# A state-space mixer on one core: where the second gate product, the step sizes' product and ScalarE's exponentials stand in the order

## The chip, the cores and the metric

The kernel runs on one core of one Trainium2 chip. A core has five engines with queues of their own: TensorE (PE in the profile; its weight loads are PEld), VectorE (DVE), ScalarE (ACT), GpSimd (POOL) and SyncE (SP, which issues the DMAs here). The metric is the device time of one launch in microseconds (us). Products are written to PSUM, from where DVE or ACT copy them out.

## The reference

One layer of attention over 32x32 tokens, a layer of two state-space mixers (forward and backward), and a spectral convolution. The change lies in the mixers, each of which computes this, for 8 sequences of 1024 tokens:

```python
def _mamba3(x, in_proj, conv_w, conv_b, A_log, dt_bias, D, norm_w, out_proj):
    zxbcdt = x @ in_proj
    z, xbc, dt = jnp.split(zxbcdt, [D_INNER, D_INNER + CONV_DIM], axis=-1)
    xp = jnp.pad(xbc, ((0, 0), (K - 1, 0), (0, 0)))
    conv = sum((xp[:, i:i + l, :] * conv_w[:, i] for i in range(K))) + conv_b
    xbc = jax.nn.silu(conv)
    xh, Bm, Cm = jnp.split(xbc, [D_INNER, D_INNER + D_STATE], axis=-1)
    dt = jax.nn.softplus(dt + dt_bias)
    A = -jnp.exp(A_log)
    y = _ssd(xh, dt, A, Bm, Cm) + xh * D[None, None, :, None]
    yg = y.reshape(b, l, D_INNER) * jax.nn.silu(z)
    yn = yg * jax.lax.rsqrt(jnp.mean(yg * yg, -1, keepdims=True) + EPS) * norm_w
    return yn @ out_proj
```

`_ssd` works in chunks of 64 tokens: decays are exponentials of differences of running sums of dt*A, each chunk's state is B times the decayed x, the states are passed on from chunk to chunk, and y is a sum of the product within the chunk and that with the state before it.

## The kernel before

All is in float32. The mixer stage is a loop over 16 units: sequence b = 0 to 7, and in each direction d = 0 (forward, the even units) and d = 1 (backward, the odd ones). The order of the instructions on every engine is the order in which the program writes them (`manual_schedule` with all engines in order), so an instruction that waits holds all behind it on its engine. One pass of the loop handles three units at once: it ends the one before (`last`), does the core of the present one (`u`), and prepares the next (`following`).

The steps of a pass, by the names that the profile shows, in the order before the change:

- `take_decays(following)`: the exponentials of the next unit's running sums (tiles cums, rest, dec, L817 to L823), and five DMAs on SP that spread them (lm and ec from cd). `between(u, Exp)`: the exponentials of lm (L857), 128x2048 in two halves.
- `turn_x(u)`: x is transposed on PE (sx, L954), and DVE multiplies it by the step sizes (xdt). `turn_b(u)`: B is transposed and multiplied with C on PE (sb, L971), and ACT copies both out (bg, L979).
- In an even unit with a sequence b+1 still to come (`fresh`), `turn_tokens` transposes its normalized tokens (px) and ACT copies them (bxt, L475).
- `project_x`/`copy_x` for the next unit, two halves: products pp on PE (L870), copies xp on ACT (L890). `gate(last)`: y times the gates on DVE, squares on ACT (L1092).
- `decayed_x(u)`, `weigh_decays(u)` on DVE (xdd, lm). `end(last)` on PE: the out-projection spo (L1099), the square sums misc (L1111) and their turn (L1125); from these rms_v on DVE, rms on POOL (L1129), and `scale_rows` on ACT (L1137), eight instructions that read spo.
- `steps(fresh)`: the step sizes, a generator that the loop advances: product pd on PE (L493), softplus in pieces on DVE and ACT (sp_v, sp_e, sp_u, sp_l), then dt and da.
- `project_z`/`activate_z`, two halves: products pz, gates zs on ACT with Silu (L916). `chunk_states` (pst, L1001), `pass_states` on DVE (state, L1018) with four DMAs (moved).
- `convolve` (three taps on DVE for each half, L903), `from_row` (lm on POOL, L848), `activate_x` (Silu on ACT, L908), `between(following, Relu)` (L857), `project_bc` (pb, L925) and `activate_bc` (bt and ct, L941). `outputs(u, 0)` and `outputs(u, 1)`: y, in two halves (sy, L1066), with the decays `add_decays` (pdec) of the unit after next between them in even units.
- In odd units the tokens of sequence b+2 are normalized (`normalize`, `normalized`: b_shift on DVE, ln_x on ACT, L460).

PSUM is handed out in two pools of two halves each[...]: `ps_w` for sx, sb, px, pp, pd, pz, pb and pdec, `ps_s` for spo, misc, pst and sy. A new tile takes a half only when the last reader of the tile before in it is done:

```python
        ps_w = s.enter_context(tc.tile_pool(name="b_ps_w", bufs=2, space=PSUM))
        ps_s = s.enter_context(tc.tile_pool(name="b_ps_s", bufs=2, space=PSUM))
```

[...]a load (ACT_TABLE_LOAD) stands where the function changes between Silu, Exp and Ln.

Of the kernel before, what the change touches and what calls it, by code (L numbers as in the profile page):

```python
# [45 lines left out]
def fast_kernel(ctx: ExitStack, tc: tile.TileContext, a: dict, out: bass.AP, bad: bass.AP):  # L46
# [431 lines left out]
    def steps(b, seq, pd):  # L478

        xt = seq["xt"]

        def small(tag):
            return tokens.tile([P, NT, n2], F32, tag=tag, name=f"{tag}{b}")

        def wide(t):
            return t.rearrange("p d h -> p (d h)").unsqueeze(1).to_broadcast([P, NT, n2])

        pd = pd[:, : NT * n2].rearrange("p (j h) -> p j h", j=NT)
        for j in range(NT):
            nc.tensor.matmul(  # L493
                pd[:, j, :],
                lhsT=xt[:, pad + j * P : pad + (j + 1) * P],
                rhs=wdt.rearrange("p d h -> p (d h)"),
                start=True,
                stop=True,
            )
        v = small("sp_v")  # L500
        nc.vector.tensor_tensor(v, pd, wide(dtb), ALU.add)
        e = small("sp_e")
        nc.vector.tensor_scalar(e, v, -1.0, None, ALU.mult)
        nc.vector.tensor_tensor(e, e, v, ALU.min)
        nc.scalar.activation(e, e, AF.Exp)
        yield
        u = small("sp_u")
        nc.vector.tensor_scalar(u, e, 1.0, None, ALU.add)  # L508
        lg = small("sp_l")
        nc.scalar.activation(lg, u, AF.Ln)  # L510
        yield
        nc.vector.scalar_tensor_tensor(u, u, -1.0, e, ALU.add, ALU.subtract)
        nc.vector.tensor_tensor(lg, lg, u, ALU.subtract)
        dt = small("dt")
        nc.vector.scalar_tensor_tensor(dt, v, 0.0, lg, ALU.max, ALU.add)
        da = tokens.tile([P, 2, NH, NT], F32, tag="da", name=f"da{b}")
        nc.vector.tensor_tensor(
            da.rearrange("p d h j -> p j d h"),
            dt.rearrange("p j (d h) -> p j d h", d=2),
            nega.unsqueeze(1).to_broadcast([P, NT, 2, NH]),  # L520
            ALU.mult,
        )
        seq["dt"], seq["da"] = dt, da
# [4 lines left out]
    with ExitStack() as s:  # L528
# [182 lines left out]
        for n in range(len(units) + 2):  # L711
# [28 lines left out]
            elif n in (103, 119):  # L740
                norming = normalized(n // 112, bridge, *norm)
                next(norming)
            elif n in (105, 122):
                next(norming, None)
            elif n == 113:
                turn_tokens(0, seqs[0], ps_t.tile([P, T], F32, tag="t", name="px0"))
            elif n == 117:
                sizes = steps(0, seqs[0], ps_t.tile([P, T], F32, tag="t", name="pd0"))
                next(sizes)
            elif n in (121, 123):  # L750
                next(sizes, None)
        assert not [*mixing, *making, *going, *coming]
# [9 lines left out]
    with ExitStack() as s:  # L762
# [431 lines left out]
        for at, u in enumerate(units):  # L1194
# [4 lines left out]
            early_decays = after_it and u.d == 1  # L1199
            if following and u.d == 1:  # L1200
                turn_decays(following)
            if at == 0:
                between(u, AF.Relu, 1.0)
            if following:
                take_decays(following)
            between(u, AF.Exp, -1.0)
            turn_x(u)
            weigh_start(u, u.convolved)
            if last:
# [1 line left out]
            turn_b(u)  # L1211
            if fresh:
                turn_tokens(fresh, seqs[fresh], wide_psum(ps_w, f"px{fresh}"))
            if following:
                project_x(following, 0)
                copy_x(following, 0)
# [3 lines left out]
            if following:  # L1220
                project_x(following, 1)
                copy_x(following, 1)
            if early_decays:
                add_decays(after_it)
            decayed_x(u)
            weigh_decays(u, 0)
            if last:
                end(last)
            if early_decays:
                turn_decays(after_it)  # L1230
            if following:
# [4 lines left out]
            norm = None  # L1236
            if u.d == 1 and b < B:
                norm = normalize(bridge, b, later=True)
            going = iter(())
            if fresh:  # L1240
                going = steps(fresh, seqs[fresh], wide_psum(ps_w, f"pd{fresh}"))
                next(going)
            weigh_decays(u, 1)
            if following:
                convolve(following, 0, range(pad - 1))
            next(going, None)
            for n in range(2):
                project_z(u, n)
                activate_z(u, n)
            if following:  # L1250
                first_tap(following, 1)
            if norm:
# [6 lines left out]
            chunk_states(u)  # L1259
            pass_states(u)  # L1260
            next(going, None)
            norming = normalized(b, bridge, *norm) if norm else iter(())
            next(norming, None)
            if stored:
                reload(stored)
            stored = None
            if following:
                convolve(following, 0, range(pad - 1, pad))
                activate_x(following, 0)
                between(following, AF.Relu, 1.0)  # L1270
                project_bc(following)
                activate_bc(following)
                convolve(following, 1)
            outputs(u, 0)
            if after_it and not early_decays:
                add_decays(after_it)
            if following:
                activate_x(following, 1)
            next(norming, None)
            outputs(u, 1)  # L1280
            if last:
                add_rows(last)
# [1076 lines left out]
```

## Time and profile before

| | us |
|---|---|
| median of 3 runs | 1477.29 |
| lowest, highest run | 1474.59, 1480.68 |
| the profiled execution | 1471.66 |
| its span, first to last instruction | 1469.9 |
| PE busy in it | 1340.2 (91%) |
| DVE busy | 1095.4 (75%) |
| ACT busy | 912.9 (62%) |
| POOL busy | 505.9 (34%) |

The mixer's first unit begins with its turned x (sx) at 474.3 us of the span, the last one's at about 1009. The mean granted clock of PE over the span is 0.978 of full speed. Busy times of PE overlap within the engine and are no measure of its distance from its peak; what its queue waits for is told by the list of waits, where each line has the waiting engine, tile and line, what it waited for, the sum, the number of waits and the longest. In lines in order of time the first two numbers are start and duration in us, the arrow points from what is read to what is written, and the brackets give the idle time before and what ended it. "issue" is a wait for which the profile shows no cause.

### The profile page before, as it was taken

To read this page: it belongs to the slowest core of one execution; us is meant where nothing else is said; L and a number is where in the kernel's file an instruction comes from. 1 tells how busy PE (TensorE), PEld (TensorE's weight loads), DVE (VectorE), ACT (ScalarE), POOL (GpSimd) and SP (SyncE) were. 2 spreads that over 40 slices of the span, in tenths; PEclk is the share of its full clock that TensorE was granted. 3 is DMA by queue.
4 is the path that set the end of the run, shared out by engine and by line. 5 is a ranking of instruction groups with operands and counts; after the bars stand their busy time and mean duration, and the time that the engine had idled before them with its cause. 6 is when DMAs were issued, how large, how long until landed. Compare 5 with 4: busy or idle time off the path is not lost. (4 is left out here: it accounts for less than half of the span.)

```text
span 1469.9 us, 45286 instructions
## 1 busy us (share of the span) xinstructions
PE 1340.2 (91%) x19782; PEld 841.3 (57%) x19782; DVE 1095.4 (75%) x2138; ACT 912.9 (62%) x1421; POOL 505.9 (34%) x510
## 2 busy tenths in 40 slices
PE   5999999999998889998989899998599899999977
PEld 2323333333333556665656566655489899999963
DVE  6788888788767687878787877787555577777755
ACT  3766666766765777777777777666355455555520
POOL 3336966866201332323232323233186211111100
PEclk9999999999999999999999999999799999999989
DMA  7101111110002334444444444341258422322258
GB/s 182 35 1 30 44 36 37 51 50 9 8 1 58 74 73 98 92 91 96 90 95 90 92 91 97 88 90 29 69 191 218 128 76 68 91 71 76 68 144 322
DMA packets 139382, 123.09 MB, mean 84 GB/s; under 512 B 44808, under 2 KB 118152, under 8 KB 135080
## 3 DMA queue, kind: packets, MB, share of 16 engines
q1 hardware_dynamic: 137064, 115.93, 30.8%
q10 hardware_dynamic: 2112, 4.19, 0.7%
q8 instruction: 157, 2.57, 0.7%
q14 instruction: 49, 0.40, 0.1%
HBM read 78.15 MB, written 34.08 MB: 76 GB/s over the span
## 5 line engine op out<-in xcount | busy, mean ns | idle before, releaser
L633 ACT ACTIVATE pr<-pt 128x1024 f32<-128x1024 f32 x256 | 247.9, 1021 | 114.3 <-PE pt L628 112.7
L658 DVE TENSOR_TENSOR two<-pr,pr 128x1024 f32<-128x1024 f32 x128 | 162.8, 1312 | 20.7 <-ACT pr L633 19.8
L1433 ACT COPY gs<-pg 128x512 f32<-128x512 f32 x256 | 132.5, 602 | 63.4 <-PE pg L1420 47.5
L1431 DVE COPY gs<-pg 128x512 f32<-128x512 f32 x256 | 158.8, 684 | 14.1 <-PE pg L1420 8.9
L628 PE MATMUL pt<-q,k 32*128 32x512 f32 x1024 | 159.3, 653 | 7.0 <-ACT pr L633 4.7
L1420 PE MATMUL pg<-taps,mst 32*128 32x128 f32 x4096 | 145.2, 280 | 4.4 <-ACT gs L1433 3.5
L1420 PEld LDWEIGHTS pg<-taps,mst 32*128 32x128 f32 x4096 | 133.3, 188 | 16.4 <-issue 11.4
L649 PE MATMUL po<-pr,v 128*32 128x512 f32 x1024 | 139.3, 602 | 0.0
L925 PE MATMUL pb<-bxt,wbc 128*128 128x512 f32 x256 | 115.6, 604 | 14.7 <-ACT zs L916 14.7
L1454 PE MATMUL py<-gs,u 128*32 128x128 f32 (+1 forms) x4096 | 127.8, 277 | 0.2 <-DVE gs L1431 0.2
L861 POOL TENSOR_TENSOR ec<-ec,ct 128x2048 f32<-128x2048 f32 x16 | 72.6, 4536 | 153.1 <-ACT ct L941 141.0
L903 DVE SCALAR_TENSOR_TENSOR xs<-xp,cw,xs 128x1024 f32<-128x1024 f32 x96 | 121.8, 1282 | 4.6 <-issue 1.7
L1454 PEld LDWEIGHTS py<-gs,u 128*32 128x32 f32 (+1 forms) x4096 | 112.0, 140 | 7.5 <-DVE gs L1431 0.4
L1443 POOL TENSOR_SCALAR u<-u 128x512 f32<-128x512 f32 x16 | 24.0, 1497 | 227.2 <-DMA u<-ud 120.1
L628 PEld LDWEIGHTS pt<-q,k 32*128 32x128 f32 x1024 | 47.6, 186 | 85.5 <-issue 32.3
L1129 POOL TENSOR_TENSOR rms<-rms_v,mhalf 128x8 f32<-128x8 f32 x16 | 27.9, 1742 | 187.5 <-DVE rms_v L1127 187.5
L925 PEld LDWEIGHTS pb<-bxt,wbc 128*128 128x128 f32 x256 | 47.7, 191 | 73.1 <-issue 59.1
L1018 DVE SCALAR_TENSOR_TENSOR state<-state,dec,pst 128x64 f32<-128x64 f32 x448 | 87.3, 275 | 1.1
L848 POOL TENSOR_TENSOR lm<-cs,lm 128x2048 f32<-128x2048 f32 x16 | 57.9, 3621 | 60.6 <-DVE sp_u L508 30.8
L649 PEld LDWEIGHTS po<-pr,v 128*32 128x32 f32 x1024 | 27.7, 109 | 88.2 <-issue 84.1
L1099 PE MATMUL spo<-wo,y 128*128 128x128 f32 x512 | 71.0, 288 | 7.9 <-DVE y L1091 7.8
L957 DVE TENSOR_TENSOR xdt<-sx,dt 128x1024 f32<-128x1024 f32 x32 | 37.9, 1220 | 52.9 <-PE sx L954 52.9
(278 smaller groups left out, 2797.9 us busy)
## 6 DMA issues: line engine op xcount, KB each, us to landing
lm<-cd SPq DMA_DIRECT2D x32, 512.0 KB
ec<-cd SPq DMA_DIRECT2D x32, 512.0 KB
ud<-sp SPq DMA_DIRECT2D x8, 1024.0 KB
u<-ud SPq DMA_DIRECT2D x32, 256.0 KB
yd<-sums SPq DMA_DIRECT2D x32, 256.0 KB
moved<-state SPq DMA_DIRECT2D x48, 128.0 KB
yt<-yd SPq DMA_DIRECT2D x6, 1024.0 KB
X<-in_x SPq DMA_DIRECT2D x8, 512.0 KB
```

What stands on the lines that cost most here:

```text
L628: nc.tensor.matmul(pt[:, i, :], lhsT=k[rows, j * P : (j + 1) * P], rhs=q[rows, cols], start=True, stop=True)
L633: nc.scalar.activation(pr[:, 2 * g : 2 * g + 2, :].rearrange("p i t -> p (i t)"), pt.rearrange("p i t -> p (i t)"), AF.Exp, scale=SCALE,)
L649: nc.tensor.matmul(po[rows, :], lhsT=vs[b][:, j, rows], rhs=pr[:, h, :], start=(j == 0), stop=(j == NT - 1))
L658: nc.vector.tensor_tensor(two, sums["pr"][:, 2 * g : 2 * g + 2, :], pr[:, 2 * g : 2 * g + 2, :], ALU.add)
L861: t = nc.gpsimd.tensor_tensor(u.ec, u.ec, u.ct.unsqueeze(1).to_broadcast([P, NH, NT, L]), ALU.mult)
L903: u.convolved = nc.vector.scalar_tensor_tensor(acc, xp[:, at : at + T], cw[u.d][:, n, i : i + 1], acc, ALU.mult, ALU.add)
L925: nc.tensor.matmul(u.pb[:, i * 512 : (i + 1) * 512], lhsT=wbc[u.d][:, k, :], rhs=xt[:, at : at + 512], start=(k == 0), stop=(k == KC - 1),)
L1018: nc.vector.scalar_tensor_tensor(u.state[:, k, h, :], u.state[:, k - 1, h, :], u.dec[:, c, h, j : j + 1], u.pst[c][:, j, h, :], ALU.mult, ...
L1420: nc.tensor.matmul(pts[g][:, e, :], lhsT=mst[rows, n * 4 + e, :], rhs=taps[rows, cols].rearrange("p f q m i -> p (f q m i)"), start=True, ...
L1431: nc.vector.tensor_copy(to, frm)
L1433: nc.scalar.copy(to, frm)
L1454: nc.tensor.matmul(py[t * 32 : t * 32 + 32 - 16 * m, q // 2, :], lhsT=u[:, i, m:, :, :, q * FC + f].rearrange("p k b i -> p (k b i)"), rhs ...
```

## The change

Four things move; nothing is added or removed.

- `steps` gets two more stops, so that its product, DVE's first three operations and ACT's exponential can stand at three places. The product now follows the second `project_x`/`copy_x`, the DVE operations follow `weigh_decays(u, 0)`, the exponential follows `end(last)`, the next piece `weigh_decays(u, 1)`.
- In units with a fresh sequence the exponentials (`take_decays`, `between(u, Exp)`) stand behind `turn_b` and `turn_tokens`.
- The second half of the gates (`project_z(u, 1)`, `activate_z(u, 1)`) moves from ahead of the states to between the two halves of the outputs.
- Around it: Relu of lm ahead of `project_bc`, `activate_x(following, 0)` behind `activate_bc`, in odd units one tap ahead of the states and five behind (before, two and four), and the whole of `normalized` behind the second `activate_x`.

```diff
@@ steps
                 stop=True,
             )
+        yield
         v = small("sp_v")
         nc.vector.tensor_tensor(v, pd, wide(dtb), ALU.add)
         e = small("sp_e")
         nc.vector.tensor_scalar(e, v, -1.0, None, ALU.mult)
         nc.vector.tensor_tensor(e, e, v, ALU.min)
+        yield
         nc.scalar.activation(e, e, AF.Exp)
         yield
@@ the attention's loop
                 sizes = steps(0, seqs[0], ps_t.tile([P, T], F32, tag="t", name="pd0"))
-                next(sizes)
+                for _ in range(3):
+                    next(sizes)
@@ the mixer's loop
-            if at == 0:
-                between(u, AF.Relu, 1.0)
-            if following:
-                take_decays(following)
-            between(u, AF.Exp, -1.0)
+
+            def decays():
+                if at == 0:
+                    between(u, AF.Relu, 1.0)
+                if following:
+                    take_decays(following)
+                between(u, AF.Exp, -1.0)
+
+            if not fresh:
+                decays()
             turn_x(u)
             weigh_start(u, u.convolved)
...
             turn_b(u)
             if fresh:
                 turn_tokens(fresh, seqs[fresh], wide_psum(ps_w, f"px{fresh}"))
+                decays()
...
                 project_x(following, 1)
                 copy_x(following, 1)
+            going = iter(())
+            if fresh:
+                going = steps(fresh, seqs[fresh], wide_psum(ps_w, f"pd{fresh}"))
+                next(going)
             if early_decays:
                 add_decays(after_it)
             decayed_x(u)
             weigh_decays(u, 0)
+            next(going, None)
             if last:
                 end(last)
+            next(going, None)
...
-            going = iter(())
-            if fresh:
-                going = steps(fresh, seqs[fresh], wide_psum(ps_w, f"pd{fresh}"))
-                next(going)
             weigh_decays(u, 1)
+            next(going, None)
+            soon = 1 if u.d else pad - 1
             if following:
-                convolve(following, 0, range(pad - 1))
-            next(going, None)
-            for n in range(2):
-                project_z(u, n)
-                activate_z(u, n)
+                convolve(following, 0, range(soon))
+            project_z(u, 0)
+            activate_z(u, 0)
...
             next(going, None)
-            norming = normalized(b, bridge, *norm) if norm else iter(())
-            next(norming, None)
...
             if following:
-                convolve(following, 0, range(pad - 1, pad))
-                activate_x(following, 0)
                 between(following, AF.Relu, 1.0)
+                convolve(following, 0, range(soon, pad))
                 project_bc(following)
                 activate_bc(following)
+                activate_x(following, 0)
                 convolve(following, 1)
             outputs(u, 0)
+            project_z(u, 1)
+            activate_z(u, 1)
             if after_it and not early_decays:
                 add_decays(after_it)
             if following:
                 activate_x(following, 1)
-            next(norming, None)
+            for _ in normalized(b, bridge, *norm) if norm else ():
+                pass
             outputs(u, 1)
```

## The prediction

> **What bounds the kernel now.** I read the stages first, then the waits of TensorE (PE) in the stage that the change touches, then single units in order of time. The page's slices put the attention ahead of about 470 us, the mixer from 470 to 1040 and the spectral stage behind it. Only the mixer's order changes (in the attention the same instructions leave at the same step), so only these 16 units count. Busy times and waits there:
>
> ```profile
> 693.00:731.00 38.00, 33.89 (x509) 23.24 (x508) 28.74 (x60) 28.09 (x44) 9.86 (x5) 1.00 0.39 88
> 731.00:765.00 34.00, 30.74 (x486) 20.59 (x485) 28.84 (x68) 25.72 (x45) 11.73 (x9) 1.00 0.39 91
> ...
> PE pb L925 <- ACT zs L916: 14.7, 15, 1.7
> PE sy L1066 <- issue: 13.4, 10, 2.5
> PE pp L870 <- ACT bg L979: 8.8, 6, 3.1
> PE sx L954 <- ACT xs L908: 7.7, 11, 1.9
> PE sb L971 <- DVE xdt L957: 6.2, 14, 0.4
> ```
>
> The first two lines are an even unit (d=0) and an odd one; after the window come its length and the busy time of PE, its weight loads, DVE, ACT and POOL, then PE's clock. PE is the longest queue (34 of 38 us, 31 of 34), no other passes 85%. So the stage lasts as long as PE's work plus PE's waits: 51 us in the five rows, some 3% of the program. The change aims at rows one to three. The question is which wait ends next behind each. For that, one even unit on ACT and on PE:
>
> ```profile
> 689.90 1.28 ACT L817 ACT_TABLE_LOAD   x1
> 692.01 2.01 ACT L857 ACTIVATE lm<-lm 128x1024 f32<-128x1024 f32 x2
> 694.04 1.01 ACT L979 COPY bg<-sb 128x1024 f32<-128x1024 f32 x1
> 694.95 1.02 ACT L475 COPY bxt<-px 128x1024 f32<-128x1024 f32 x1
> 697.13 1.01 ACT L890 COPY xp<-pp 128x1024 f32<-128x1024 f32 x1 [1.16 <-PE pp L870]
> 704.93 2.18 ACT L1137 ACTIVATE y<-spo,rms 128x128 f32<-128x128 f32 x8 [1.75 <-POOL rms L1129]
> ...
> 695.11 3.71 PE L870 MATMUL pp<-bxt,win 128*128 128x512 f32 x8 [1.30 <-ACT bg L979]
> 702.52 0.38 PE L1125 MATMUL misc<-ident,sums 128*128 128x128 f32 x2
> 703.63 1.85 PE L493 MATMUL pd<-wdt,bxt 128*128 128x8 f32 x16
> 705.34 3.69 PE L870 MATMUL pz<-bxt,win 128*128 128x512 f32 x8
> 708.96 1.98 PE L1001 MATMUL pst<-xdd,bg 64*64 64x128 f32 x64
> 712.67 1.56 PE L925 MATMUL pb<-bxt,wbc 128*128 128x512 f32 x3 [1.74 <-ACT zs L916]
> ```
>
> ACT's copy of bg stands behind load and exponentials (load to last exponential 4.12 us) and holds pp for 1.30; pb waits 1.74 for the gates; between the end of the scaled rows (707.11) and pst lie only 1.85 us. How close that is, a unit without pd shows:
>
> ```profile
> 991.61 2.18 ACT L1137 ACTIVATE y<-spo,rms 128x128 f32<-128x128 f32 x8 [2.66 <-POOL rms L1129]
> ...
> 993.84 1.96 PE L1001 MATMUL pst<-xdd,bg 64*64 64x128 f32 x60 [0.46 <-ACT y L1137]
> ```
>
> pst, after two of its 32 products, waits until the scaled rows are out of the other half of that PSUM pool. At 959.90 the same shows as a pst of 2.50 in place of 1.98.
>
> [...]the trace has 1.28, right before the activation that needs it, so it moves along with the exponentials.[...] In the DMA view single 16 KB packets of queue q8 do lie in PE's issue gaps (684.0 to 684.5, 757.0 to 757.5)[...]. [...]after the issue gap of 1.94 at 614 the clock is 0.70 and 0.87 in two windows of 4 us, after 2.45 at 757 it stays 1.00.
>
> **The change part by part.** E is the end of sb, T the end of pst. Even unit with a fresh sequence (seven: 0, 2 to 12), times from the unit at 692.78 = E, T = 710.94 = E+18.16.
>
> *Exponentials behind turned B.* bg now starts at E+0.05 and pp no longer waits: 1.3 less. But the next x's copy is behind the exponentials: bg to E+1.06, bxt to 1.98, load and exponentials 4.12 to 6.1, first xp copy to 7.14. Its PSUM half is what pd, two tiles later, takes over.
>
> *Step sizes' product behind the next x.* px, then pp from E+1.1 to 4.75 (2 x 1.83), then pd: it waits to E+7.2, **a new wait of 2.4 us**. With pd's 1.72 the out-projection spo starts at E+8.92; before at E+5.87 (698.65), with pd still to come: net +1.3. On DVE rms_v and the second lm stand behind sp_v, which waits for pd to E+9.0; rms_v is due at E+13.3, so nothing is late. On PE, spo and all that follows stand behind pd. The five loads that SP issues for the exponentials leave 5 us later; before they flowed from 694 to 704, so now to 709, and POOL's lm at 710 finds them there.
>
> *Gates' second product out.* From spo's start the square sums' turn comes 3.87 later (E+12.79), and rms_v, POOL's 1.64 and eight row scalings end 4.59 after that: E+17.38. PE gets there sooner: spo 4.98, one pz 1.81, so E+15.7. **pst waits 1.65 us for the rows**, then runs 1.96: T = E+19.4, 1.2 later than before. This cover of 3.55 us (pd and one pz) was what hid the rows.
>
> *Behind T, even.* pb 7.07, half the outputs 2.02, pz 1.83, pdec 1.12, other half 2.16, turn 0.17: sx starts at T+14.3, ends at T+16.4; before T+17.04. pb has its PSUM half from pd, so its 1.74 is gone. DVE has the last tap at T+11.83, ACT is through lm (now ahead of pb), B and C, gates, x at T+13.4: nobody holds sx. The new place of the gates makes ACT wait for pz, to T+10.95, in front of x's second half; DVE delivers that at T+11.83, so the wait is covered. Gain 0.67. An even unit is **+0.56**.
>
> *Odd units* (E = 730.50, T = 746.04). The rows end at 743.93 as before; pz was hiding them by 0.13. Now pst waits 1.6 and T gains 0.1. Then PE could reach sx at T+12.95 (7.05, 2.02, 1.83, 2.05). DVE: states to T+5.88, then five taps (one more than before, as only one goes ahead of pst) of 1.26 to T+12.25, ACT's x to T+13.4, sx done at T+15.27. Before, b_shift and ln_x stood in front of ACT's x and B and C, and sx ended at T+16.13. The ln_x go behind it, and end at about T+16.6, before px at T+17.7. **-0.96**. The issue gap, 1.0 to 2.45 in these units, was covered by ACT's chain (ACT's x ends 760.26, the gap 759.72). It should shrink[...].
>
> First unit: no rows yet; exponentials plus 2 us of Relu hold pd to 488.95, T is 494.45 against 495.18, then the 0.67: -1.4. Unit 13 -0.4 (its sx ended at T+15.66), unit 14 -0.6 (T+15.55 to T+14.95), the last +0.4 (z's product inside its outputs).
>
> Sum: -1.4 + 6 x 0.56 - 6 x 0.96 - 0.4 - 0.6 + 0.4 = **-4.4 us**.
>
> *What the trace of before doesn't show* is what the clock does around pd's wait: 2.4 us idle, then 1.7 us of products eight columns wide. Below: 0 (3.06 idle before pp in the first unit, clock 1.00). Above: 1.7 in each of seven units, 12 us (sx took 3.70 for 2.07 after the gap at 614; 4 x 0.30 + 4 x 0.13 = 1.7). Gaps of 1.8 to 2.45 among small products did it in two of five. I take one or two of seven, +2.4. It can't go below nothing: no clock here is above 1.00.
>
> **Forecast**: -2 us, no change. The profiled execution took 1471.66 (span 1469.9), the median is 1477.29; the same step from the median gives 1475.
>
> **Rivals.** *The copy of x isn't held* (faster): were ACT to take xp ahead of the exponentials, or pd another PSUM half, even units lose the 2.4 again and the first 4.3: -4.4 - 14.4 - 4.3 = -23, 1454. For it speaks only that ACT is idle 1.2 us before bg, where a load could go; against it that every load follows directly on the activation before it and both queues keep the program's order. *The rows don't hold pst*: units 13 and 14 speak against it; it would give some 1.5 more per unit, and lands near the same time. *The clock falls* (slower): at pd in all seven units and at half of 13 pst waits, 13 x 1.7 - 4.4 = +18, 1495. It decides from the 7th drop on (7.4 + 4.4 over 1.7). For it: the stretch from pp's end to spo is 4.2 us with thin work[...]; after 3.46 idle us of 3.95 at 1013.87 spo and misc did slow. Against it: the waits of 1.74 before pb never did it. *The issue gap stays* at 1.5 in odd units: sx ends at T+16.5, not 15.27: some +8, total +4, within what is no change.
>
> **How the numbers follow.** Forecast case 0.58 (its own range 1467 to 1484), copy not held 0.17, clock 0.25. About 0.5% (7.4 us) is what a measurement here can tell from no change. The forecast case gives faster 0.17, same 0.38, slower 0.03; the copy's case is faster; of the clock's 0.22 is slower and 0.03 same. Faster 0.34, same 0.41, slower 0.25. The range goes halfway into both rivals: 1458 to 1492.
>
> **What would show it.** In the waits, pb <- ACT zs and pp <- ACT bg gone; new pd <- ACT xp of about 2.4 in even units and pst <- ACT y of about 1.6 in thirteen; the issue row down to a few us; sx <- ACT xs about 0.4 in odd units; clock below 0.9 between pd and spo in one or two. I am wrong if pd doesn't wait, or if even units get shorter than 37.7 us from sb to sb.

## The result, and the profile after

The changed kernel takes 1499.32 us (median of 4 runs, 1495.96 to 1501.40); the kernel before took 1478.30 beside it (4 runs, 1474.59 to 1480.68). The ratio is 1.0147, with a 95% interval of 1.0124 to 1.0171: slower by 21 us, where 1475 and no change were forecast, and above the range.

From the end of the first unit's sb to that of the last the profiled execution takes 558.8 us against 534.1 before, +24.8 (the whole spans differ by 28.7: 1498.6 against 1469.9). First the windows of an even unit and of an odd one, from sb to sb, then three stretches within the even one; the columns are those of the windows shown of before:

```profile
703.76:744.86 41.10, 35.70 (x508) 24.56 (x508) 28.44 (x59) 30.89 (x48) 11.76 (x10) 0.96 0.35 79
744.86:778.67 33.81, 31.64 (x485) 20.78 (x485) 29.02 (x68) 23.25 (x38) 12.60 (x9) 1.00 0.41 95
711.00:713.00 2.00, 2.00 (x18) 2.00 (x19) 0.76 (x2) 2.00 (x3) 0.00 (x0) 1.00 1.08 258
713.00:715.00 2.00, 2.00 (x12) 2.00 (x11) 0.54 (x3) 0.66 (x1) 0.00 (x0) 0.51 0.95 205
715.00:717.00 2.00, 2.00 (x22) 1.35 (x21) 0.00 (x0) 0.00 (x0) 0.00 (x0) 0.64 1.10 238
```

The odd units became shorter: 33.15 to 33.9, where most took 34.20. The six even units with a fresh sequence, the first apart, take 40.8 to 42.4 against 36.5 to 37.7 before, +26.8 together; the first unit and units 13 and 14 lose 4.3 more, and the odd ones give back 6.4. The last three lines are what a sum of busy times hides: PE is 100% busy in all three, yet its clock (the third number from the end) falls from 1.00 to 0.51 as the out-projection begins. The list of PE's waits in the mixer:

```profile
PE pst L1004 <- ACT y L1140: 26.0, 15, 2.5
PE pd L493 <- ACT xp L893: 18.3, 7, 4.4
...
PE sy L1069 <- issue: 1.8, 3, 0.8
```

pb's wait for the gates (14.7 before) and pp's for bg (8.8) are gone, the issue row fell from 13.4 to 1.8. In their place stand two rows that the change made. The even unit in order of time, on ACT, PE, DVE and POOL:

```profile
705.85 1.28 ACT L820 ACT_TABLE_LOAD   x1
707.95 2.00 ACT L860 ACTIVATE lm<-lm 128x1024 f32<-128x1024 f32 x2
709.86 0.99 ACT L893 COPY xp<-pp 128x1024 f32<-128x1024 f32 x1
721.92 2.18 ACT L1140 ACTIVATE y<-spo,rms 128x128 f32<-128x128 f32 x8 [2.86 <-POOL rms L1132]
...
704.87 3.71 PE L873 MATMUL pp<-bxt,win 128*128 128x512 f32 x8
710.91 1.95 PE L493 MATMUL pd<-wdt,bxt 128*128 128x8 f32 x16 [2.33 <-ACT xp L893]
712.72 3.49 PE L1102 MATMUL spo<-wo,y 128*128 128x128 f32 x16
...
719.36 1.89 PE L873 MATMUL pz<-bxt,win 128*128 128x512 f32 x4
721.18 0.44 PE L1004 MATMUL pst<-xdd,bg 64*64 64x128 f32 x4
724.15 1.96 PE L1004 MATMUL pst<-xdd,bg 64*64 64x128 f32 x60 [2.53 <-ACT y L1140]
...
719.18 1.22 DVE L1043 TENSOR_TENSOR lm<-lm,bg 128x1024 f32<-128x1024 f32 x1
...
719.34 2.54 POOL L1132 TENSOR_TENSOR rms<-rms_v,mhalf 128x8 f32<-128x8 f32 x1 [15.37 <-DVE rms_v L1130]
```

Two lines of before that compare with these:

```profile
698.65 1.95 PE L1099 MATMUL spo<-wo,y 128*128 128x128 f32 x16
...
703.26 1.64 POOL L1129 TENSOR_TENSOR rms<-rms_v,mhalf 128x8 f32<-128x8 f32 x1 [11.25 <-DVE rms_v L1127]
```

Load, exponentials, copy of x, then pd after 2.33 us of idleness: the new wait is there as worked out. But the first 16 products of spo take 3.49 in place of 1.95, POOL's rms takes 2.54 in place of 1.64, and so the scaled rows end at 724.10 and pst waits 2.53.

### The profile page after: what moved, and what is told of

It reads as the page before. It is cut to its first block, busy times and chain, and to the rows that moved or that the text cites. A ratio compares the mean times of both kernels' runs of the same rounds, so it can differ in the third digit from the quotient of the medians.

```text
span 1498.6 us, 45320 instructions
## 1 busy us (share of the span) xinstructions
PE 1367.2 (91%) x19782; PEld 857.2 (57%) x19782; DVE 1095.2 (73%) x2138; ACT 916.6 (61%) x1421; POOL 522.6 (35%) x510
## 3 DMA queue, kind: packets, MB, share of 16 engines
q8 instruction: 157, 2.57, 0.7%
## 5 line engine op out<-in xcount | busy, mean ns | idle before, releaser
L864 POOL TENSOR_TENSOR ec<-ec,ct 128x2048 f32<-128x2048 f32 x16 | 84.0, 5250 | 160.1 <-PE pz L873 93.3
L1132 POOL TENSOR_TENSOR rms<-rms_v,mhalf 128x8 f32<-128x8 f32 x16 | 33.3, 2083 | 219.1 <-DVE rms_v L1130 219.1
L1102 PE MATMUL spo<-wo,y 128*128 128x128 f32 x512 | 80.4, 313 | 7.9 <-DVE y L1094 7.8
L1102 PEld LDWEIGHTS spo<-wo,y 128*128 128x128 f32 x512 | 72.2, 221 | 16.3 <-issue 11.4
L860 ACT ACTIVATE lm<-lm 128x1024 f32<-128x1024 f32 x64 | 64.0, 1048 | 15.8 <-POOL lm L851 15.5
```

Of the source, the lines that this page charges most:

```text
L1102: nc.tensor.matmul(u.po[:, j, :], lhsT=u.y[:, n, j * P : (j + 1) * P], rhs=wo[u.d][:, n, :], start=(n == 0), stop=(n == 1),)
```

## The experiments

Three theories stood after the result: (a) *pd's new place lowers the clock*, by its wait for the copy of x, its thin products (eight columns wide), or both; (b) *the scaled rows lost their cover*, so pst waits; (c) *the gates' second product* is what fails. Each diff is against the changed kernel unless said otherwise; lines left out of a diff are marked by three dots; medians are of 4 runs, of 6 for `pd_back`, 7 for `gates_alone` and 20 for `x_ahead`; the kernel before ran beside each (1474.6 to 1475.5).

### One move undone at a time

`exp_back`, the exponentials ahead of the turned x in all units; `pd_back`, the step sizes' product back behind `scale_rows`; `gates_back`, both halves of the gates ahead of the states; `gates_alone`, the first two together.

```diff
# exp_back
-            if not fresh:
-                decays()
+            decays()
...
-                decays()
# pd_back
-            going = iter(())
-            if fresh:
-                going = steps(fresh, seqs[fresh], wide_psum(ps_w, f"pd{fresh}"))
-                next(going)
...
+            going = iter(())
+            if fresh:
+                going = steps(fresh, seqs[fresh], wide_psum(ps_w, f"pd{fresh}"))
+                for _ in range(3):
+                    next(going)
             weigh_decays(u, 1)
# gates_back
-            project_z(u, 0)
-            activate_z(u, 0)
+            for n in range(2):
+                project_z(u, n)
+                activate_z(u, n)
...
-            project_z(u, 1)
-            activate_z(u, 1)
```

> The changed kernel with one part undone: ScalarE's exponentials stand ahead of the turned x again in every unit; step sizes' product and gates stay moved. Theory A (the order of ScalarE's copies makes pd wait, and the wait brings PE's clock down): the 2.33 us that pd waits for the copy of xp is gone in all seven even units, the out-projection spo after it takes 5.15 us again in place of 6.8, pp waits 1.3 for bg again; even units some 2.7 us shorter, in all about -20 us against the changed kernel, near 1480. pst still waits about 2.2 for the scaled rows. Rival B (pd's early place is what costs, wherever the exponentials stand): pd or spo still waits about 2 us, and the time stays above 1493.

> The changed kernel with one part undone: the step sizes' product pd and its softplus stand ahead of the second weighing of lm again; exponentials and gates stay moved. Theory A: nothing waits for the copy of xp, but the square sums misc now wait about 2.5 us for the squares that ScalarE makes behind the exponentials (end of sb plus 9.1 us); pd stands between spo and pst again and hides the scaled rows, so pst waits no more, and POOL's rms runs beside an idle DVE in 1.64 in place of 2.54. Even units 36.7 to 38.4 us in place of 42, in all -25 to -35 us against the changed kernel, 1465 to 1475. Rival (the exponentials' place is the loss): no better than 1490.

> The changed kernel with one part undone: both halves of the gates' product stand ahead of the states again; exponentials and pd stay moved. Theory A: pst no longer waits in odd units and only some 0.4 us in even ones, but pb waits for the gates again (about 1.8 in even units, 0.4 in odd) and the odd units lose the 1 us that they had gained; the clock's drops at pst go; the pd wait and its drop stay. In all between -5 and +8 us against the changed kernel, 1494 to 1507. Rival (the waits of pst for the scaled rows are the main loss): -20 us or more, below 1480.

> The changed kernel with two parts undone: exponentials and pd where they were before, only the gates' second product (and the small moves around it) stays between the outputs. Theory A: bg holds pp for 1.3 again, pd hides the scaled rows in even units, odd units keep their gain of 1 us and their 1.2 us wait of pst: even units about 35.2 us, odd 33.2, the mixer some 24 us shorter than before the change, 1450 to 1460: faster than both kernels. Rival (the gates' new place is itself at fault): not faster than 1478.

`pd_alone` undoes the exponentials and the gates together, so that of the three moves only pd's is left:

> The changed kernel with the exponentials ahead of the turned x again in every unit, and with both halves of the gates ahead of the states: of the three moves only that of the step sizes' product is left. Theory (the product was cover for the scaled rows, and the gates' second half was the other cover): in even units pst waits some 0.5 and at the most 1.2 in place of 2.2, no clock drop at pst; spo runs 5.2 in all units; what is paid is the wait of pp for bg of some 2.6 in seven units, which is there because the next tokens' normalisation now stands behind x on ScalarE, and pb waits 1 for the gates: 1478 to 1486, faster than with the gates' half moved too (1488.8). Rival (the product is worse at this place whatever stands around it, as thin work next to idle time): spo or misc run more than 1.5 us longer in half of the even units, 1488 or more.

| kept of the three moves | label | us | ratio to before, 95% |
|---|---|---|---|
| none (the kernel before) | | 1474.6 | |
| gates | gates_alone | 1470.16 | 0.9963, 0.9948 to 0.9979 |
| gates, exponentials | pd_back | 1468.38 | 0.9958, 0.9941 to 0.9975 |
| pd | pd_alone | 1492.78 | 1.0114, 1.0087 to 1.0142 |
| gates, pd | exp_back | 1488.78 | 1.0098, 1.0073 to 1.0123 |
| exponentials, pd | gates_back | 1502.11 | 1.0172, 1.0148 to 1.0197 |
| all | the changed kernel | 1499.32 | 1.0147, 1.0124 to 1.0171 |

Every kernel of this table with pd behind the next x is slower than before, every one without it faster. Theory (c) falls: in none of the three pairs that differ by the gates do they lose. The medians gain 4.4, 4.0 and 2.8 us, the last two within the intervals (the first pair differs by the small moves around the gates too, which no run takes alone). The exponentials behind B gain 2 us without pd's move, within the intervals, and cost 7 (by the ratios) to 10 (by the medians) with it; pd's move costs 19 without them and 28 to 31 with them. `gates_back` came as expected in its time: pst waits 0.46 in even units and pb again for the gates, 14.2 in all. `pd_back` has no wait of pst in them; its misc waits for the squares (10.8 in 12 places), as these stand behind the copies on ACT, and in two of the six spo took 1.6 longer behind that wait.

Why `exp_back` is still slow, in its even unit:

```profile
698.40 3.71 PE L873 MATMUL pp<-bxt,win 128*128 128x512 f32 x8 [2.42 <-ACT bg L982]
701.95 1.85 PE L493 MATMUL pd<-wdt,bxt 128*128 128x8 f32 x16
703.65 2.03 PE L1102 MATMUL spo<-wo,y 128*128 128x128 f32 x16
...
713.50 0.77 PE L1004 MATMUL pst<-xdd,bg 64*64 64x128 f32 x19 [2.53 <-ACT y L1140]
```

pd follows pp without a gap and spo runs at full speed in every unit; for (a), this says that pd's 1.85 us of thin products alone did not lower the clock here. But pp waits 2.4 to 2.7 for bg, twice the 1.3 of before, because the next tokens' ln_x now stands behind x on ACT. In four of six units pp then took 5.1 to 6.7 for its 3.71. The rows still hold pst for 2.2 to 2.5, as (b) says, and in five of six pst and pb behind it then took 1.6 us longer. `gates_alone` missed its 1450 to 1460 by the same wait of pp and a pp of 5.40 behind it in four of six, and had even units of 35.6 to 38.3.

`pd_alone` fulfilled the first half of its expectation (pst waits 0.46 in every even unit, spo 5.23) and missed the time. The waits of pp and pb were in it; what neither theory named is what stood behind them. In its even unit:

```profile
777.80 5.40 PE L873 MATMUL pp<-bxt,win 128*128 128x512 f32 x8 [2.84 <-ACT bg L982]
...
794.23 1.96 PE L1004 MATMUL pst<-xdd,bg 64*64 64x128 f32 x60 [0.46 <-ACT y L1140]
798.13 8.83 PE L928 MATMUL pb<-bxt,wbc 128*128 128x512 f32 x16 [1.94 <-ACT zs L919]
```

pp waits 2.84 and then takes 5.40 for its 3.71; pst is followed by a wait of 1.94 for the gates, which on ACT stand behind the rows and two table loads for the softplus, and pb takes 8.83 for its 7.14. Each of these two waits cost 1.7 more in the products behind it: at pp in four of six units (2.9 in one of them), at pb in all six.

### pd's gap and the clock

`pp_twice` fills the gap: in units with a fresh sequence it computes the second half of pp twice (1.8 us of wide products that the kernel doesn't need).

```diff
                 project_x(following, 1)
+                if fresh:
+                    for i in range(2):
+                        nc.tensor.matmul(following.pp[:, i * 512 : (i + 1) * 512], ...)
                 copy_x(following, 1)
```

> The changed kernel with work added: in the seven even units with a fresh sequence, the second half of the next x's product pp is computed twice, into the same place (1.83 us more of PE work, inside the 2.33 us that pd waits). Theory A (the wait brings PE's clock down, and spo and misc after it pay): the gap before pd shrinks to some 0.5 us, spo takes 5.15 us again in place of 6.8, and the time falls by some 1.6 us in each of seven units, about -11 us against the changed kernel, near 1488, though more is computed. Rival B (the clock falls for another reason, or the long spo has another cause): spo stays at 6.8 and the time stays within 4 us of the changed kernel.

1497.33, ratio 1.0140 (1.0102 to 1.0177). An even unit of it:

```profile
705.83 1.88 PE L1233 MATMUL pp<-bxt,win 128*128 128x512 f32 x4
708.32 1.95 PE L493 MATMUL pd<-wdt,bxt 128*128 128x8 f32 x16 [0.61 <-ACT xp L893]
710.13 3.66 PE L1102 MATMUL spo<-wo,y 128*128 128x128 f32 x16
```

The gap was 0.61 as expected, but spo ran 6.83 in four of six even units and 5.23 in two, and the 11 us of the theory did not come. A short gap with thin products behind it still did it, though not always.

`x_ahead` shortens the gap without more work: only the two exponentials of lm, and DVE's first weighing with them, go behind the out-projection. `no_gap` moves the load and the small exponentials too, behind the first copy of x and the squares.

```diff
# x_ahead
             def decays():
...
-                between(u, AF.Exp, -1.0)
             if not fresh:
                 decays()
+                between(u, AF.Exp, -1.0)
...
-            weigh_decays(u, 0)
+            if not fresh:
+                weigh_decays(u, 0)
...
             if last:
                 end(last)
+            if fresh:
+                between(u, AF.Exp, -1.0)
+                weigh_decays(u, 0)
# no_gap, as well
             if fresh:
                 turn_tokens(fresh, seqs[fresh], wide_psum(ps_w, f"px{fresh}"))
-                decays()
...
                 gate(last, 1)
+            if fresh:
+                decays()
```

> The changed kernel with one thing moved: in units with a fresh sequence the two exponentials of lm (2.0 us), and DVE's first weighing of lm with them, go behind the out-projection; the load and the small exponentials stay behind the turned B. Then the first copy of the next x ends 2.0 us sooner (at about E+5.2 for 7.1), just after the next x's product (E+4.8), and pd's wait falls from 2.33 to about 0.35 in seven units, while everything else of the change stays: pst's wait for the scaled rows of about 2.2 in even units, rms of about 2.5 where DVE weighs lm beside it. Theory (the time that pd's wait and its clock drop take is what the forecast missed): the stretch of wait and pd is 2.3 us and makes no drop in most units, spo runs 5.2 in at least five of seven, even units fall from 41.9 to about 38.3, time 1472 to 1478, near the kernel before. Rival (pd's thin products alone lower the clock, or the clock drops at pst's wait in their place): spo above 6.5 in three or more of seven, or pst above 6 in most even units; even units stay above 40, time above 1485.

> As x_ahead, but in units with a fresh sequence the load and the small exponentials also leave the place behind the turned B and stand behind the first copy of the next x and the squares. The first copy then starts as soon as its half of pp is out (about E+2.9) and is done at about E+4, before pp ends at E+4.8, so pd follows pp with no gap. pd itself, its 1.85 us of products eight columns wide and its place stay. Theory (gap and thin products together lower the clock: 0.44 + 1.95 did it in six of six, 1.85 alone in none of the kernels whose pd follows pp directly): spo runs 5.2 in all units, misc 1.07, even units fall from 38.13 to about 36.1 (0.44 of gap, 1.6 of clock), time about 1458. Rival (pd's thin products at this place lower the clock by themselves, and only a wait of pp ahead of them kept those other kernels free of it): spo stays at 6.8 in most even units, which then fall by the gap alone to about 37.7, time about 1468.

`x_ahead`: 1471.10, ratio 0.9965 (0.9955 to 0.9976). The time is the theory's, the clock is the rival's: pd waits 0.44 in each, and spo still runs 6.8 in six of six. Its even unit in windows (PE's clock third from the end), from pp to spo's first products:

```profile
693.00:695.40 2.40, 1.97 (x5) 0.57 (x3) 2.40 (x3) 2.33 (x7) 0.00 (x0) 1.00 0.06 14
695.40:697.30 1.90, 1.89 (x17) 1.89 (x17) 1.53 (x2) 1.90 (x3) 0.00 (x0) 1.00 0.32 121
697.30:699.30 2.00, 2.00 (x13) 2.00 (x13) 0.65 (x3) 0.99 (x2) 0.00 (x0) 0.62 1.08 229
```

Most of the 28 us against the changed kernel is the rest: 1.9 less of pd's wait, and DVE's lm no longer over the start of rms, which took 1.63 again, so that pst waits 1.44 in place of 2.2 and never runs slowly behind it in the six. `no_gap` in the same place:

```profile
690.59 3.71 PE L873 MATMUL pp<-bxt,win 128*128 128x512 f32 x8
694.14 1.85 PE L493 MATMUL pd<-wdt,bxt 128*128 128x8 f32 x16
695.84 2.03 PE L1102 MATMUL spo<-wo,y 128*128 128x128 f32 x16
...
704.73 1.96 PE L1004 MATMUL pst<-xdd,bg 64*64 64x128 f32 x60 [1.57 <-ACT y L1140]
```

1461.92, ratio 0.9900 (0.9873 to 0.9928). With the last 0.44 us of gap gone, nothing waits ahead of pp, pd is where the change put it, and spo runs 5.23 in all; even units fall from 38.1 to 35.96. That settles (a) for these runs: gap and thin products *together* lowered the clock (0.44 and 1.95 us, in six of six units of `x_ahead`); the 1.85 us of pd alone did not, nor did a short gap alone (pp of before waits 0.53 in one unit, pb 0.37 in most odd ones, at a clock of 1.00). It also shows that pd's place is no loss in itself: with the copy of x ahead of the exponentials the change as a whole gains.

Why a gap did it in four units of `pp_twice` and not in two, its trace shows. In the profiles the clock changes only on a grid of windows of 3.41 us, which lies differently in each run (before and after it reads 1.00 or 0.50, and all 27 of its changes before and all 43 after lie whole multiples of 3.41 apart). An even unit with a slow spo (the first two lines) and one with a fast spo, cut along the grid:

```profile
631.75:635.16 3.41, 2.80 (x24) 2.63 (x24) 2.11 (x5) 3.41 (x4) 0.00 (x0) 1.00 1.02 250
635.16:638.57 3.41, 3.41 (x23) 2.50 (x26) 0.07 (x1) 0.12 (x1) 0.00 (x0) 0.50 0.99 211
556.65:560.07 3.42, 2.81 (x9) 1.02 (x8) 3.42 (x4) 3.40 (x5) 0.00 (x0) 1.00 0.31 74
560.07:563.48 3.41, 3.41 (x32) 3.40 (x31) 1.15 (x4) 2.50 (x3) 0.00 (x0) 1.00 1.05 233
563.48:566.89 3.41, 3.41 (x37) 2.72 (x36) 0.81 (x2) 1.66 (x3) 0.56 (x1) 1.00 1.00 216
```

In the first, gap and pd lie within one window, which leaves 1.00 us of other products in it, and the next window runs at half clock. In the second a boundary cuts them, the two windows keep 2.56 and 1.85 us of other products, and the clock stays. Over the mixer of all 15 profiles the windows at full clock divide like this:

| products other than pd in a window | windows | next one at half clock |
|---|---|---|
| under 1.5 us | 81 | 81 |
| 1.5 to 1.72 us | 36 | 14 |
| over 1.72 us | 2135 | 1 |

Of these windows 160 are from the kernel before (next at half clock: 4 of 4, none of 6, none of 150) and 156 from the changed one (12 of 12, 2 of 2, none of 142). In them pd counted like idle time, and the next clock went with how much other work was left in one window. The six of six of `x_ahead` are then not six independent cases: two of its units together take 71.3 to 71.9 us, 21 windows take 71.68, so the boundary fell at nearly the same place each time. `no_gap` is no such luck: in 12 units of it, `exp_back` and `pd_alone` pd lay whole within one window, and the clock stayed.

### The scaled rows

`rms_alone` lets DVE do both weighings of lm before the out-projection's sums are out, in units with a fresh sequence, and holds DVE's taps until rms is done. `pst_split` turns the order of pst's products: all those of chunk half 0, which write the PSUM half that is free, then all of half 1, which waits for the rows.

```diff
# rms_alone
             weigh_decays(u, 0)
+            if fresh:
+                weigh_decays(u, 1)
...
-            weigh_decays(u, 1)
+            if not fresh:
+                weigh_decays(u, 1)
...
-                convolve(following, 0, range(soon))
+                convolve(following, 0, range(1))
+                if fresh and last:
+                    behind(following.convolved, last.rms, "behind the rows' scale")
+                convolve(following, 0, range(1, soon))
# pst_split, in chunk_states
-            for j in range(NT) if u.d == 0 else reversed(range(NT)):
-                for c in range(2):
+            for c in range(2):
+                for j in range(NT) if u.d == 0 else reversed(range(NT)):
```

> The changed kernel with DVE kept idle while POOL computes rms in the six even units that have one: the second weighing of lm goes ahead of the step sizes' DVE operations, and the taps ahead of the states wait for rms. Theory A (POOL's rms takes 2.54 in place of 1.64[...]): rms takes 1.64 again, the scaled rows end 0.9 earlier, pst waits 1.3 in place of 2.2 in these units, -5 us against the changed kernel, and up to -14 if the shorter wait also spares the clock's drops at pst. Rival B (rms is longer for the data or for another reason): rms stays 2.54 and the time rises by up to 3 us.

> The changed kernel with the states' products pst in another order: first all 16 products into the half of PSUM that is free, then the 16 into the half that the scaled rows still hold (before, the third product waited). Theory A (only the second half's tile waits for the rows): 14 more products, 0.87 us, go ahead of the wait; pst waits 1.3 in place of 2.2 in even units and 0.3 in place of 1.2 in odd ones: -0.9 us in 15 units, -13 us against the changed kernel, near 1486, more if the clock then stays up. Rival B (both halves wait): no change.

`rms_alone`, DVE and POOL in its even unit:

```profile
711.07 2.35 DVE L1043 TENSOR_TENSOR lm<-lm,bg 128x1024 f32<-128x1024 f32 x2
721.00 0.17 DVE L1130 TENSOR_SCALAR rms_v<-misc 128x8 f32<-128x8 f32 x1 [5.65 <-PE misc L1128]
...
721.25 1.63 POOL L1132 TENSOR_TENSOR rms<-rms_v,mhalf 128x8 f32<-128x8 f32 x1 [16.65 <-DVE rms_v L1130]
```

rms takes 1.63 in all six, against 2.54 beside DVE's lm: the 0.9 came with the work beside it. It came where lm covers the start of rms (in the changed kernel lm begins 0.16 ahead of it); in `x_ahead` lm begins 0.6 to 1.1 us into rms, and rms stays 1.63. pst then waits 1.27, and its products run at full speed in all six. The time stayed, 1498.57, ratio 1.0142 (1.0104 to 1.0181), because pd (up to 3.5) and spo (7 to 8) lost more to the clock than in the changed kernel (10.4 together for 8.8): even units 41.5 against 41.9.

`pst_split`, an even unit and an odd one:

```profile
720.97 1.96 PE L1004 MATMUL pst<-xdd,bg 64*64 64x128 f32 x32
723.93 1.96 PE L1004 MATMUL pst<-xdd,bg 64*64 64x128 f32 x32 [1.00 <-ACT y L1140]
756.50 3.60 PE L1004 MATMUL pst<-xdd,bg 64*64 64x128 f32 x64
```

The wait fell to between 0 and 1.0, but the 32 records of one half took 1.96, as long as all 64 in the given order, and the odd unit's pst took the same 3.6 as with its wait. Time 1496.37, ratio 1.0151 (1.0109 to 1.0193): nothing gained. Theory (b) is right about the wait, which pd's old place covers (none in the even units of `pd_back`); but at pd's new place, making the wait shorter gained nothing by itself.

### A version that beats both

`combined` starts from `pd_back`: squares ahead of the copies of x and the exponentials of lm behind the out-projection, in units with a fresh sequence, one tap ahead of the states everywhere, and pst's turned order. `combined_joined` has pst's given order. `decays_cover` moves, on top of that, the decays of the unit after next behind the out-projection in odd units.

```diff
# combined and combined_joined, beside pd_back and x_ahead
                 project_x(following, 0)
-                copy_x(following, 0)
+                if not fresh:
+                    copy_x(following, 0)
...
                 gate(last, 1)
             if following:
+                if fresh:
+                    copy_x(following, 0)
                 project_x(following, 1)
...
-            soon = 1 if u.d else pad - 1
+            soon = 1
# decays_cover, beside combined_joined
-            if early_decays:
-                add_decays(after_it)
             decayed_x(u)
...
             if early_decays:
-                turn_decays(after_it)
+                add_decays(after_it)
...
             project_z(u, 0)
+            if early_decays:
+                turn_decays(after_it)
```

> A version put together from the measured parts: gates between the outputs; step sizes' product back ahead of pst, where it covers the scaled rows; in fresh units ScalarE takes the squares of y ahead of the copies of the next x, and the exponentials of lm behind the square sums' copy; pst in the split order; one tap ahead of the states in every unit. Theory A: neither pp, pd, misc nor pst has a wait over 0.5 us, even units about 34.5 us and odd ones 32.3, so some -35 us against the kernel before, 1440. Rival (another wait takes their place, ScalarE's queue being the likeliest: table loads, exponentials and scaled rows in one row): between 1450 and 1470.

> As the combined kernel, but with the states' loop in its given order (both halves of a chunk next to each other). In the combined kernel the rows of the last unit are out at about E+13.4 in even units and pst starts at E+13.3, so the other order bought nothing there and its 3.34 us in place of 1.98 were paid in full. Theory (order of the products sets their speed): pst 1.98 again in even units, 35.33 becomes 34.0 for each, odd units stay at 33.15 because a wait of 1.2 for the scaled rows comes back. Sum -1.3 x 7 = -9: about 1449, and no clock drop, as waits of 1.2 have made none so far. Rival (the waits come back and the clock falls): pst waits more than 1.8 in even units, they stay above 35.3, time 1458 or more.

> As combined_joined, and in odd units the decays of the unit after next (pdec, 1.0 us of small products) go from ahead of the out-projection to behind it, their turn to behind the first gates' product. In front of the out-projection they cover nothing; behind it they stand where pst waits for the scaled rows. Theory (pst's wait is the time from the out-projection to the rows, 1.65 of POOL and 2.2 of ScalarE in it, less the products in between): pst's wait of 1.2 in the seven odd units falls to about 0.2, odd units go from 33.15 to about 32.2, -6 us against combined_joined: about 1443. Rival (DVE's gates or squares hold the out-projection if it comes 1 us sooner): misc or spo waits by 0.5 to 1 and no more than 3 us are gained.

`combined` takes 1457.99, ratio 0.9886 (0.9837 to 0.9935), not the 1440 of its theory: pst in the turned order takes 3.34 in its even units, which are 35.33 long. `combined_joined` takes 1451.45, ratio 0.9832 (0.9795 to 0.9868), near the 1449 of its theory. An even unit of it, 34.15 long:

```profile
693.71 1.95 PE L1102 MATMUL spo<-wo,y 128*128 128x128 f32 x16
...
698.69 1.85 PE L493 MATMUL pd<-wdt,bxt 128*128 128x8 f32 x16
700.40 1.97 PE L873 MATMUL pz<-bxt,win 128*128 128x512 f32 x4
702.30 2.15 PE L1004 MATMUL pst<-xdd,bg 64*64 64x128 f32 x64
```

pd and one pz stand where the rows are awaited, and none of these lines waits. `decays_cover` gave no more, where 1443 was expected: 1450.40, ratio 0.9837 (0.9807 to 0.9866). Its odd unit on ACT shows why:

```profile
593.33 0.26 ACT L807 COPY cums<-pdec 32x128 f32<-32x128 f32 x1 [2.92 <-PE pdec L805]
593.49 0.22 ACT L809 COPY dsum<-pdec 128x96 f32<-128x96 f32 x1
593.62 1.24 ACT L898 ACTIVATE xs<-xp,cb,cw 128x1024 f32<-128x1024 f32 x1
594.77 2.09 ACT L1140 ACTIVATE y<-spo,rms 128x128 f32<-128x128 f32 x8
```

rms was done at 593.33, but ACT took the two copies of the moved decays and a tap first, and the rows began 1.44 later; pst waited 1.28, where it had waited 1.20. The rival had named DVE; it was ACT's queue.

## Why the prediction was wrong, point by point

**The step that failed** is the one on "what the clock does around pd's wait": "I take one or two of seven, +2.4". It was seven of seven. The price of 1.7 was right (spo 6.81 to 6.92 for 5.15 to 5.24, in the first unit pd 3.50 for 1.85), the count was wrong: some 11.6 us where 2.4 was put. The prediction named pd's thin products, but took the share from gaps alone, "two of five". In the runs pd counted like idle time: 0.44 of gap and 1.95 of pd did it in six of six, 0.61 and 1.95 in four of six, 2.33 and 1.95 in all, pd without a gap in none. Gap and pd of the change are 4.28 us together; wherever the boundary of a window falls, one window then holds at least half of them and keeps at most 1.27 us (3.41 less 2.14, an estimate from these figures) of other products, and under 1.5 was followed by half clock in 81 of 81. So seven of seven was not bad luck. The trace of before agrees: of the five gaps that the prediction counted, the two with 1.94 and 2.26 us in one window lowered the clock, those with 1.82, 1.70 (of 2.45) and 0.95 (of 1.88) did not.

**The second, smaller one** is "pst waits 1.65 us for the rows". The place was right and the time too short, for one term: from pst's start to the end of the rows it measured 2.57 in five of the six even units and 2.92 in one, where rms_v came 0.35 later. (The lists show 2.18 and 2.53, as 0.44 of it goes into pst's first products.) Spo's 1.7 of clock moves rows and pst alike and cancels; "POOL's 1.64" was 2.54, because DVE weighs lm beside it, where before DVE had been held up by pd. Units 13 and 14 of before already show 2.48 for rms, with lm beside it; the prediction quoted 991.61 from there and read only the wait. At this longer wait the clock fell in three of six (pst 6.04 to 6.16 for 4.58), which the forecast case counted at nothing.

The six even units together grew by 26.8 where 3.4 was forecast. Of the 23.5 between: 6 x 1.67 = 10.0 spo with the square sums between its parts, 6.1 the longer stretch from pst's start to the rows, 4.6 pst's clock, 1.6 pd once slow itself, less 0.8 behind T: 21.5. The other 2.0 is that two of the six had been shorter than 37.7 before (36.95, 36.51). The first unit was +2.2 where -1.4 was forecast, units 13 and 14 were +2.1 together where -1.0 was: at pst's waits of 1.81 and 2.19 the clock fell too.

**What was right.** pd's wait: 2.4 forecast, 2.33 measured, 4.36 in the first unit. Both rows of waits gone; the issue row down, 13.4 to 1.8 (by what, was not shown); odd units 34.2 - 0.96 = 33.24 forecast, 33.15 to 33.9 measured, with 1.58 from pst's start to the end of the rows for the 1.6. Behind T an even unit took what was worked out, 18.75 for 18.9. The slower rival, "the clock falls", 1495, had the mechanism and pd's seven units right. That its number came near is in part luck: of pst's waits five of fifteen lowered the clock, none of them at the 1.20 of the odd units up to unit 11, where it had half of 13. What spoke against it in the prediction, the waits of 1.74 before pb that never did it, carried too far: a wait of 1.94 at that place did, in six of six units of `pd_alone` and two of six of `gates_back`.

The rival "the copy of x isn't held" had 1454, for a case in which the exponentials do not stand ahead of the copy; `no_gap` is near to that case and took 1461.92, still with pst's waits.

## What to carry to other kernels

A product that seems out of place may be the cover of a latency elsewhere: before moving it, list what ran beside the time that it takes, here the chain from sums over rms to scaled rows, and name what will cover that instead. Price a new wait in front of thin products not by its length alone: add the thin work to it, ask how much other work a window of the clock's grid (3.41 us in these profiles) can still hold around both (here under 1.5 us was followed by half clock in 81 of 81), and reckon with slower products behind them (here 3.49 us for 1.95). When a wait goes on one engine, look at what the engine that had been held will now run beside (here lm beside rms, 2.54 us for 1.64).

## What of the hardware was not expected

- The clock fell behind less idleness than the gaps of 1.8 to 2.45 us that the prediction counted. In `x_ahead` 0.44 us idle and 1.95 us of products eight columns wide, 2.4 together, were enough in six of six, and the window of 2 us behind them reads 0.62 in the unit shown. On the grid of 3.41 us, under 1.5 us of other products in a window was followed by half clock in 81 of 81, over 1.72 once in 2135, the one in `combined`, where pst runs one chunk half at a time. So the same wait did it in one unit and not in the next, by where the grid fell: waits of 1.2 to 1.6 ahead of pst did it in none of 89 (in the changed kernel, none of 7), waits of 1.8 to 2.5 in 21 of 37 (in the changed kernel, 5 of 8). What exactly lowers the clock, no run here shows.
- rms on POOL, 128 x 8 numbers, took 1.63 without lm beside it (`rms_alone`) and 2.48 to 2.54 where DVE's lm times bg, 1.22 us long, covered its start: 0.8 to 0.9 more. Why, no run here shows.
- pst's 64-row products took 1.98 for 64 records where the two chunk halves alternate (before), and 1.96 for 32 where one half runs alone (`pst_split`). The cause is not shown.
